# Score rounds of a fused attention and feed-forward block: two heads' plain scores beside two heads' lowered scores

## The chip, the cores and the metric

The kernel runs on one core of one Trainium2 chip. The core has five engines with a queue each: PE (matrix products into PSUM), DVE (vector work), ACT (activations), POOL (vector work[...]) and SP, which issues most of the transfers. The metric is the time of one execution in microseconds (us); lower is better. Times are medians of several executions.

## The reference

One block of a transformer in float32: four sequences (B) of 512 rows (T) of width 512 (D), 32 query heads of 16 columns that share 8 key and value heads, and a gated feed-forward layer of width 1376. Queries and keys are rotated by position, scores are causal, and the softmax is the usual one with its maximum taken off.

```python
q = q * cos + _rotate_half(q) * sin
k = k * cos + _rotate_half(k) * sin
att = jnp.einsum('bhgqd,bhkd->bhgqk', qg, k) / math.sqrt(D_HEAD)
att = jnp.where(causal, att, -jnp.inf)
probs = jax.nn.softmax(att, axis=-1)
ctx = jnp.einsum('bhgqk,bhkd->bhgqd', probs, v)
...
x = x + attention(_layernorm(x))          # with Wq, Wk, Wv, Wo
y = _layernorm(x)
x = x + (jax.nn.silu(y @ W_gate.T) * (y @ W_up.T)) @ W_down.T
```

Wq and Wk are drawn eight times larger than the other weights, so the scores are large and their maxima must be taken off before the exponential.

## The kernel before

**Groups.** The attention is cut into 32 groups of four heads (`GROUPS`, eight for each of the four sequences): pairs of groups (`hf` 0 and 1) share a tile of 128 query columns. The four heads of a group lie on partitions 0 to 31, 32 to 63, 64 to 95 and 96 to 127, so that their products, of 32 rows each, take separate quarters of PE. `masked(g)` (L436, POOL) makes the tile `qa[g]`: the group's rotated queries with one half of each 32 rows zeroed. The keys carry a row of ones in the zeroed half (L277), so whatever is written to that row of `qa` is added to each score of the query.

**Two passes over the scores.** The plain scores (L451, queries on the partitions of PSUM) serve to find each query's maximum. Their negatives are put into the spare row of `qa`, and the lowered scores (L549, keys on the partitions) then come out with the maximum already taken off. Exponentials (L556, ACT), a select that zeroes what lies above the diagonal (L560, POOL), and the products with the values (`averages`, L578) follow. The values carry ones beside them, so the sums of the softmax come out of the same products; `low_half`, `high_half`, `inverse` and `reciprocal` (L588 to L602) divide by them once per pair of groups.

**Rounds.** Four PSUM banks, one per head, are held as two tiles of two banks, `pairs`. A causal group of plain or lowered scores fits in two and a half fillings of them: 512 columns; 384 and 128; 256. So a group has five rounds: lowered 512, plain 512, lowered 384+128, plain 384+128, and last lowered 256 beside plain 256. The plain scores belong to a later group `h`, the lowered ones to the current group `g`. Lowered rounds are emptied by ACT (two exponentials of 1024 columns). In plain rounds DVE takes the maxima of heads 0 and 1 from PSUM (`from_bank`, L473, with the causal mask added), while ACT copies heads 2 and 3 to SBUF (L501), POOL masks the copy (L505) and DVE reduces it (L492, `from_copy`). In the last round DVE takes all four heads from PSUM, and the exponentials are issued after it.

**Two ways for the maxima.** For groups under `NEAR` = 9 the maxima go into the wide tiles `low`; `lowered(g)` turns them with four PE transposes (L524), and DVE adds them to `qa` (L525); `h` is then `g + 1`. From group 9 on they go into `packed`, are turned in 32x32 blocks by DVE (L531, `turned_round`), written to DRAM (L532) and read back into the spare rows of `qa` by four small transfers (L541, `laid_out`); `h` is then `g + 2`.

**What lies between the rounds.** Everything else is cut into steps of some 1.7 us of PE work: projections (L235, L290), output projection (L342), the feed-forward layer (L390, L416). `slot(b, steps)` runs the eight groups of one sequence and spreads the steps over the gaps between the rounds by shares written by hand. Slot 0 is filled with projections of later sequences only; slots 1 to 3 with output projections and feed-forward layers. Work that needs no PE stands in queues which the order of the code empties: `full` (what finishes a projection in slot 0: rotation on DVE and POOL, L243 to L246), `aside` (layer norm statistics, L187 to L195, and spreading of the keys), `later` (the divisions, on DVE) and `later_act` (`low_half`, on ACT). `thin` is true in slot 0. Before slot 0 come the first sequence's projections and the first group's plain scores, with query projections (`start[6:]`) and the second sequence's transposes (`turned1`, L207) between the rounds. POOL sets the spare parts of the value tiles there (L646) after `masked(0)` (L644).

The order of instructions is the order of the code (manual schedule); the tile framework adds the waits. Each engine runs its queue in order.

Of the kernel before, what the change touches and what calls it, by code (L numbers as in the profile page):

```python
# [48 lines left out]

NEAR = 9  # L50
# [26 lines left out]
def preln_block_kernel(  # L77
# [54 lines left out]
    low = [const.tile([P, NT, P], F32, name=f"low{hf}") for hf in range(2)]  # L132


    packed = [const.tile([P, 32], F32, name=f"packed{n}") for n in range(3)]
# [24 lines left out]
    sc = [pairs[r // 2][:, r % 2, :] for r in range(4)]  # L160
# [39 lines left out]
    def do(queue, n=1):  # L200
        for _ in range(min(n, len(queue))):
            queue.popleft()()
# [239 lines left out]
    def scores(g, at):  # L442

        if g >= len(GROUPS):
            return
        k = keys_of(g)
        for i, c in at:
            for r in range(4):
                rows = slice(32 * r, 32 * r + 32)
                n = P * (i + 1)  # L450
                nc.tensor.matmul(  # L451
                    sc[r][:, c : c + n], lhsT=qa[g][rows, ts(i, P)], rhs=k[rows, :n], start=True, stop=True
                )

    def greatest(g, at, lo, hi):


        if g >= len(GROUPS):
            return
        hf = GROUPS[g][2]  # L460

        def found(head, i):
            if g < NEAR:
                row = 32 * head + 16 * (1 - hf)
                return low[hf][:, i, row : row + 1]
            return packed[g % 3][:, NT * head + i : NT * head + i + 1]

        def from_bank(pair):
            for i, c in at:
                n = P * (i + 1)  # L470
                for r in range(2):
                    junk = work.tile([P, T], F32, tag="junk", name="junk")
                    nc.vector.tensor_tensor_reduce(  # L473
                        out=junk[:, :n],
                        in0=pairs[pair][:, r, c : c + n],
                        in1=mask[:, T - n :],
                        scale=-1.0,
                        scalar=BIG,
                        op0=ALU.add,
                        op1=ALU.min,  # L480
                        accum_out=found(2 * pair + r, i),
                    )

        def from_copy():
            for i, c in at:
                n = P * (i + 1)
                if g < NEAR:
                    row = 16 * (1 - hf)
                    dst = low[hf][:, i, :].rearrange("p (r k) -> p r k", k=32)[:, 2:4, row]
                else:  # L490
                    dst = packed[g % 3][:, 2 * NT : 4 * NT].rearrange("p (r i) -> p r i", i=NT)[:, :, i]
                nc.vector.tensor_reduce(  # L492
                    dst, copy[:, :, c : c + n], axis=mybir.AxisListType.X, op=ALU.max, negate=True
                )

        if lo > 0:
            from_bank(0)
            from_bank(1)
            return
        copy = work.tile([P, 2, T], F32, tag="copy", name="copy", bufs=2)  # L500
        nc.scalar.copy(copy, pairs[1])  # L501

        late = min(c + P * i for i, c in at)
        blocks = copy[:, :, late:hi].rearrange("p r (a k) -> p r a k", k=P)
        nc.gpsimd.affine_select(  # L505
            out=blocks,
            in_=blocks,
            compare_op=ALU.is_ge,
            fill=MASKED,
            base=0,  # L510
            pattern=[[0, 2], [0, (hi - late) // P], [-1, P]],
            channel_multiplier=1,
        )
        from_bank(0)
        do(full, len(full))
        from_copy()

    def lowered(g):

        if g >= len(GROUPS):  # L520
            return
        pt = bank()
        for i in range(NT):
            nc.tensor.transpose(pt[:, ts(i, P)], low[GROUPS[g][2]][:, i, :], ident)  # L524
        nc.vector.tensor_tensor(qa[g], qa[g], pt, ALU.add)  # L525

    def turned_round(g):
        if g >= len(GROUPS):
            return
        t = small.tile([P, 32], F32, tag="turned", name="turned", bufs=2)  # L530
        nc.vector.transpose(t, packed[g % 3])  # L531
        nc.sync.dma_start(out=lowest[g % 2], in_=t)  # L532
# [10 lines left out]
    def lowered_scores(g, at):  # L543

        k = keys_of(g)
        for j, c in at:
            for r in range(4):
                rows = slice(32 * r, 32 * r + 32)
                nc.tensor.matmul(  # L549
                    sc[r][:, c : c + T - P * j], lhsT=k[rows, ts(j, P)], rhs=qa[g][rows, P * j :], start=True, stop=True  # L550
                )

    def probabilities(at, e, width):

        for n in (1, 0):
            nc.scalar.activation(  # L556
                e[:, 2 * n : 2 * n + 2, :], pairs[n][:, :, :width], AF.Exp, scale=1.0 / math.sqrt(DH)
            )
        for j, c in at:
            nc.gpsimd.affine_select(  # L560
                out=e[:, :, c : c + P],
                in_=e[:, :, c : c + P],
                compare_op=ALU.is_ge,
                fill=0.0,
                base=0,
                pattern=[[0, 4], [1, P]],
                channel_multiplier=-1,
            )
# [64 lines left out]
    for t in (*low, *packed):  # L633
        nc.gpsimd.memset(t, 0.0)
# [15 lines left out]
    rounds = (((3, 0),), 0, T), (((2, 0), (0, 3 * P)), 0, T), (((1, 2 * P),), 2 * P, T)  # L650
    thin[0] = True
    for at, steps in zip(rounds, ([*start[6:8]], [*start[8:10]], [*turned1, *rest1[:2]])):
        scores(0, at[0])
        greatest(0, *at)
        do(full, len(full))
        for cost, step in steps:
            step()
    masked(1)
    lowered(0)
    for cost, step in start[10:]:  # L660
        step()

    def fill(steps, upto, done):
        while steps and done + steps[0][0] / 2 <= upto:
            cost, step = steps.popleft()
            step()
            done += cost
        return done

    def slot(b, steps):  # L670
# [5 lines left out]
        shares = 8 + 0.5 * (NEAR - 1 in groups)  # L676
        thin[0] = b == 0

        def gap(share):
            nonlocal done, part  # L680
            part += share / shares
            done = fill(steps, total * part, done)

        for g in groups:
            h = g + 1 if g + 1 < NEAR else g + 2
            if g % 8 == 7:
                do(aside, len(aside))
            lowered_scores(g, ((0, 0),))
            probabilities(((0, 0),), e0, T)
            if g + 1 > NEAR:  # L690
                laid_out(g + 1)
            do(later)
            if not thin[0]:
                do(aside)
            gap(0.17 if thin[0] else 0.19)
            if h == NEAR + 1:
                for at, lo, hi in rounds:
                    scores(NEAR, at)
                    greatest(NEAR, at, lo, hi)
                    gap(0.17)  # L700
                turned_round(NEAR)
                laid_out(NEAR)
            at, lo, hi = rounds[0]
            scores(h, at)
            greatest(h, at, lo, hi)
            do(aside)
            gap(0.15 if thin[0] else 0.17)
            lowered_scores(g, ((1, 0), (3, 3 * P)))
            probabilities(((1, 0), (3, 3 * P)), e1, T)
            do(later_act)  # L710
            do(later)
            if not thin[0]:
                do(aside)
            gap(0.17 if thin[0] else 0.19)
            at, lo, hi = rounds[1]
            scores(h, at)
            greatest(h, at, lo, hi)
            if thin[0]:
                do(aside)
            gap(0.17 if thin[0] else 0.2)  # L720
            at, lo, hi = rounds[2]
            lowered_scores(g, ((2, 0),))
            scores(h, at)
            greatest(h, at, lo, hi)
            if h > NEAR:
                turned_round(h)
            probabilities(((2, 0),), e2, 2 * P)
            if h == NEAR - 1:
                masked(NEAR)
                masked(NEAR + 1)  # L730
            elif h < NEAR:
                masked(g + 2)
            else:
                masked(g + 3)
            do(full, len(full))
            gap(0.17 if thin[0] else 0.25)
            averages(g)
            if h < NEAR:
                lowered(h)
            if thin[0]:  # L740
                do(aside)
                gap(0.17)
# [89 lines left out]
```

## Time and profile before

| | |
|---|---|
| median of 3 runs | 988.41 us (986.64 to 991.55) |
| profiled execution, its own time | 997.9 us |
| its span, first to last instruction | 996.2 us |
| mean granted PE clock | 0.969 |
| PE busy | 924.1 us (93%) |
| DVE busy | 492.4 us (49%) |
| ACT busy | 282.1 us (28%) |
| POOL busy | 246.6 us (25%) |
| maxima from PSUM, L473 | 320 instructions: 512 columns 691 ns, 384 557, 256 424, 128 291 |
| read of a maximum behind each | 83 ns |
| exponentials, L556 | 128 of 1024 columns, 1021 ns; 64 of 512, 594 ns |
| copy of two heads, L501 | 64, 1013 ns |
| mask of the copy, L505 | 64, 640 or 423 ns |
| reductions of the copy, L492 | 1024 elements 1222 ns, 768 954, 256 411 |
| transposes of the maxima, L524, and addition, L525 | 36 of 306 ns, 9 of 688 ns |
| reciprocals, L601 | 32, 1738 ns |

How to read it: the page cuts the span into 40 equal slices and gives each engine's busy share in tenths; PEclk is the clock that PE was granted. A group line has busy time and mean duration, then the idle time of the engine just before these instructions and what ended it. Matrix products are pipelined and run four at a time in the attention, so the sum of their durations is more than their busy time. An f32 product appears as two records. In the time line each line has start, duration, engine, source line, and in brackets the idle time before it with its releaser.

### The profile page before, as it was taken

To read this page: it belongs to the slowest core of one execution; us is meant where nothing else is said; L and a number is where in the kernel's file an instruction comes from. 1 tells how busy PE (TensorE), PEld (TensorE's weight loads), DVE (VectorE), ACT (ScalarE), POOL (GpSimd) and SP (SyncE) were. 2 spreads that over 40 slices of the span, in tenths; PEclk is the share of its full clock that TensorE was granted. 3 is DMA by queue.
4 is the path that set the end of the run, shared out by engine and by line. 5 is a ranking of instruction groups with operands and counts; after the bars stand their busy time and mean duration, and the time that the engine had idled before them with its cause. 6 is when DMAs were issued, how large, how long until landed. Compare 5 with 4: busy or idle time off the path is not lost.

```text
span 996.2 us, 12538 instructions
## 1 busy us (share of the span) xinstructions
PE 924.1 (93%) x4708; PEld 407.2 (41%) x4708; DVE 492.4 (49%) x1194; ACT 282.1 (28%) x359; POOL 246.6 (25%) x358
## 2 busy tenths in 40 slices
PE   6967876888989999999899999998999999999998
PEld 3443333335334344344444444444444434444443
DVE  7455556466746464554664545365555531512110
ACT  0223323343233433332233333323242422010000
POOL 5463443346231221122211111122111111100000
PEclk9998879798989999999999999999999999999999
DMA  6100100000024421013012111010112111022100
GB/s 211 43 1 1 43 1 1 1 1 1 3 64 160 158 58 46 24 53 130 12 55 65 44 40 43 22 44 12 54 44 65 39 44 54 21 74 75 47 11 32
DMA packets 62492, 47.18 MB, mean 47 GB/s; under 512 B 11520, under 2 KB 54528, under 8 KB 62176
## 3 DMA queue, kind: packets, MB, share of 16 engines
q1 hardware_dynamic: 62144, 40.62, 14.1%
q10 hardware_dynamic: 288, 5.77, 1.5%
q8 instruction: 37, 0.61, 0.3%
q14 instruction: 23, 0.19, 0.1%
HBM read 38.92 MB, written 7.45 MB: 47 GB/s over the span
## 4 chain that ended last, share of the span: by engine, by line
PE 82%; DVE 5%; issue 5%; ACT 4%; POOL 3%; DMA 0%; ACTq 0%; POOLq 0%; DVEq 0%
PE mm L390 30%; PE mm L416 14%; PE sc L549 9%; PE sc L451 8%; PE av L578 7%; PE mm L235 6%; PE mm L342 5%; ACT e L556 4%; DVE junk L473 2%; PE mm L207 1%; PE mm L290 1%; DVE st L187 1%; DVE rot L243 1%; PE mm L524 1%; POOL e L560 1%
## 5 line engine op out<-in xcount | busy, mean ns | idle before, releaser
L390 PE MATMUL mm<-xnT,shared 128*128 128x512 f32 (+1 forms) x704 | 322.7, 604 | 0.0
L556 ACT ACTIVATE e<-sc 128x1024 f32<-128x1024 f32 (+1 forms) x192 | 158.8, 879 | 372.1 <-PE sc L549 220.2
L473 DVE CUSTOM_DVE_ANT_0 junk<-sc,mask 128x256 f32<-128x256 f32 (+3 forms) x320 | 152.7, 477 | 154.2 <-PE sc L451 126.8
L390 PEld LDWEIGHTS mm<-xnT,shared 128*128 128x128 f32 (+1 forms) x704 | 126.3, 188 | 164.5 <-issue 155.5
L560 POOL TENSOR_SCALAR_AFFINE_SELECT e<-e 128x512 f32<-128x512 f32 x128 | 80.3, 638 | 417.1 <-ACT e L556 184.6
L416 PE MATMUL mm<-wd_sb,home 128*128 128x512 f32 (+1 forms) x352 | 159.6, 600 | 0.0
L549 PE MATMUL sc<-qa,home 32*128 32x512 f32 (+3 forms) x1024 | 99.9, 483 | 15.6 <-DVE low L473 13.6
L451 PE MATMUL sc<-home,qa 32*128 32x512 f32 (+3 forms) x1024 | 95.8, 466 | 18.2 <-ACT e L556 16.3
L501 ACT COPY copy<-sc 128x1024 f32<-128x1024 f32 x64 | 64.8, 1013 | 119.1 <-PE sc L451 109.5
L416 PEld LDWEIGHTS mm<-wd_sb,home 128*128 128x128 f32 (+1 forms) x352 | 64.6, 190 | 82.8 <-issue 81.4
L578 PE MATMUL av<-e,home 128*32 128x512 f32 (+3 forms) x1024 | 79.7, 448 | 15.4 <-POOL e L560 15.4
L399 DVE SCALAR_TENSOR_TENSOR g<-g,mm 128x512 f32<-128x512 f32 (+1 forms) x44 | 30.2, 686 | 100.4 <-ACT g L398 100.4
L549 PEld LDWEIGHTS sc<-qa,home 32*128 32x128 f32 x1024 | 44.7, 190 | 83.7 <-issue 22.1
L451 PEld LDWEIGHTS sc<-home,qa 32*128 32x128 f32 x1024 | 47.3, 187 | 74.7 <-issue 27.8
L235 PE MATMUL mm<-xnT,shared 128*128 128x512 f32 x120 | 64.2, 675 | 0.8 <-issue 0.8
L505 POOL TENSOR_SCALAR_AFFINE_SELECT copy<-copy 128x256 f32<-128x256 f32 x64 | 34.0, 531 | 114.2 <-ACT copy L501 114.2
L401 DVE TENSOR_TENSOR home<-mm,g 128x512 f32<-128x512 f32 (+1 forms) x44 | 30.2, 686 | 61.6 <-PE mm L390 61.6
L492 DVE TENSOR_REDUCE packed<-copy 128x2 f32<-128x1024 f32 (+2 forms) x69 | 57.5, 862 | 5.0 <-POOL copy L505 3.0
L342 PE MATMUL mm<-wo_sb,cx 128*128 128x512 f32 x128 | 59.4, 605 | 0.0
L578 PEld LDWEIGHTS av<-e,home 128*32 128x32 f32 x1024 | 28.6, 111 | 72.7 <-issue 46.2
L601 DVE RECIPROCAL inv<-inv 128x256 f32<-128x256 f32 x32 | 55.3, 1738 | 0.1
L398 ACT ACTIVATE g<-mm 128x512 f32<-128x512 f32 (+1 forms) x44 | 26.4, 599 | 97.4 <-PE mm L390 97.4
(75 smaller groups left out, 552.6 us busy)
## 6 DMA issues: line engine op xcount, KB each, us to landing
shared<-in_wg SPq DMA_DIRECT2D x40, 256.0 KB
shared<-in_wu SPq DMA_DIRECT2D x40, 256.0 KB
xr<-in_x SPq DMA_DIRECT2D x16, 256.0 KB
out<-xr SPq DMA_DIRECT2D x16, 256.0 KB
xa<-in_x SPq DMA_DIRECT2D x12, 256.0 KB
spill<-wd_sb ACTq DMA_DIRECT2D x1, 2816.0 KB
home<-spill ACTq DMA_DIRECT2D x1, 2816.0 KB
wd_sb<-in_wd SPq DMA_DIRECT2D x1, 2560.0 KB
```

The costliest lines, as they stand in the source:

```text
L235: nc.tensor.matmul(ps, lhsT=w[:, k, ts(m, P)], rhs=xnT[:, k, :], start=k == 0, stop=k == NK - 1)
L342: nc.tensor.matmul(ps, lhsT=cx[m][:, ts(i, P)], rhs=wo_sb[:, m, :], start=m == 0, stop=m == 3)
L390: nc.tensor.matmul(ps[:m, :], lhsT=wgu[c][:, a, k, :m], rhs=xnTs[""][:, k, :], start=k == 0, stop=k == NK - 1)
L416: nc.tensor.matmul(py[i], lhsT=homes[n][:m, f, ts(i, P)], rhs=wd_sb[:m, f, :], start=f == 0, stop=f == NF - 1)
L451: nc.tensor.matmul(sc[r][:, c : c + n], lhsT=qa[g][rows, ts(i, P)], rhs=k[rows, :n], start=True, stop=True)
L473: nc.vector.tensor_tensor_reduce(out=junk[:, :n], in0=pairs[pair][:, r, c : c + n], in1=mask[:, T - n :], scale=-1.0, scalar=BIG, op0=ALU.add,
L492: nc.vector.tensor_reduce(dst, copy[:, :, c : c + n], axis=mybir.AxisListType.X, op=ALU.max, negate=True)
L501: nc.scalar.copy(copy, pairs[1])
L549: nc.tensor.matmul(sc[r][:, c : c + T - P * j], lhsT=k[rows, ts(j, P)], rhs=qa[g][rows, P * j :], start=True, stop=True)
L556: nc.scalar.activation(e[:, 2 * n : 2 * n + 2, :], pairs[n][:, :, :width], AF.Exp, scale=1.0 / math.sqrt(DH))
L560: nc.gpsimd.affine_select(out=e[:, :, c : c + P], in_=e[:, :, c : c + P], compare_op=ALU.is_ge, fill=0.0, base=0, pattern=[[0, 4], [1, P]] ...
L578: nc.tensor.matmul(av[32 * r : 32 * r + 32, P * j :], lhsT=v[:, j, 4 * (m // 2) + r, DH * (1 - hf) : DH * (3 - hf)], rhs=e[:, r, c : c + n ...
```

## The change

All groups now use the way through DRAM: `NEAR`, `lowered`, the wide `low` tiles, and the copying of heads 2 and 3 are gone; `packed` is renamed `low`. `h` is `g + 2` for every group, so the plain scores of both groups 0 and 1 are found before slot 0.

The rounds are mixed. `plain` and `less` are the two pairs of banks. In each of four visits two heads of group `h` have plain scores in `plain`, and the other two heads of group `g` have lowered scores in `less`: 512 columns for one half of the heads and then the other, and the same with 384 and 128. One exponential empties `less`, DVE's maxima (`greatest`) empty `plain`. In the fifth, `last_visit`, each bank holds 256 lowered columns and 256 plain ones, issued head by head; the exponentials are now issued ahead of the maxima. The last two groups have no `h`, and use both pairs for lowered scores.

The shares of the steps are equal: a fortieth of the slot in each of five gaps a group. In slots 1 to 3 `fill` also takes one entry of `aside` after each step. Two steps of the second sequence's queries move from slot 0 to before it, and two of the fourth sequence's move from slot 1 to slot 0. `masked(0)` at L644 is left as it is.

```diff
-    low = [const.tile([P, NT, P], F32, name=f"low{hf}") for hf in range(2)]
-    packed = [const.tile([P, 32], F32, name=f"packed{n}") for n in range(3)]
+    low = [const.tile([P, 32], F32, name=f"low{n}") for n in range(3)]
...
-    sc = [pairs[r // 2][:, r % 2, :] for r in range(4)]
+    plain, less = pairs
...
+    def both_scores(h, g, visit):
+        for c, i, j, heads in visit:
+            for r in heads:
+                if h < len(GROUPS):
+                    plain_score(h, r, i, plain[:, r % 2, c : c + P * (i + 1)])
+                else:
+                    less_score(g, r, j, plain[:, r % 2, c : c + T - P * j])
+            for r in (2, 3) if heads[0] == 0 else (0, 1):
+                less_score(g, r, j, less[:, r % 2, c : c + T - P * j])
+
+    def greatest(g, r, i, src):
+        n = P * (i + 1)
+        junk = work.tile([P, T], F32, tag="junk", name="junk")
+        nc.vector.tensor_tensor_reduce(
+            out=junk[:, :n],
+            in0=src,
+            in1=mask[:, T - n :],
+            scale=-1.0,
+            scalar=BIG,
+            op0=ALU.add,
+            op1=ALU.min,
+            accum_out=low[g % 3][:, NT * r + i : NT * r + i + 1],
+        )
+
+    def all_greatest(h, visit):
+        if h < len(GROUPS):
+            for c, i, j, heads in visit:
+                for r in heads:
+                    greatest(h, r, i, plain[:, r % 2, c : c + P * (i + 1)])
+        do(full, len(full))
+
+    def last_visit(h, g):
+        for r in range(4):
+            if h < len(GROUPS):
+                plain_score(h, r, 1, pairs[r // 2][:, r % 2, 2 * P :])
+            less_score(g, r, 2, pairs[r // 2][:, r % 2, : 2 * P])
+        for n in (1, 0):
+            exponentials(e2[:, 2 * n : 2 * n + 2, :], pairs[n][:, :, : 2 * P])
+        causal(e2, 0)
+        masked(g + 3)
+        if h < len(GROUPS):
             for r in range(4):
...
+                greatest(h, r, 1, pairs[r // 2][:, r % 2, 2 * P :])
         do(full, len(full))
...
-    rounds = (((3, 0),), 0, T), (((2, 0), (0, 3 * P)), 0, T), (((1, 2 * P),), 2 * P, T)
+    low_heads, high_heads = (0, 1), (2, 3)
+    visits = (
+        ((0, 3, 0, low_heads),),
+        ((0, 3, 0, high_heads),),
+        ((0, 2, 1, low_heads), (3 * P, 0, 3, low_heads)),
+        ((0, 2, 1, high_heads), (3 * P, 0, 3, high_heads)),
+    )
     thin[0] = True
...
+    shares = [2, 2, 2, 5, 2, 1]
+    opening = deque([*start[6:], *turned1, *rest1[:4]])
+    for h in range(2):
+        masked(h)
+        for entries in (((0, 3),), ((0, 2), (3 * P, 0)), ((0, 1),)):
+            for c, i in entries:
+                for r in range(4):
+                    plain_score(h, r, i, pairs[r // 2][:, r % 2, c : c + P * (i + 1)])
+            for r in range(4):
+                for c, i in entries:
+                    greatest(h, r, i, pairs[r // 2][:, r % 2, c : c + P * (i + 1)])
+            do(full, len(full))
+            for _ in range(shares.pop(0)):
+                opening.popleft()[1]()
+        turned_round(h)
+        if h == 0:
+            laid_out(0)
+    masked(2)
...
             done += cost
+            if not thin[0]:
+                do(aside)
...
         for g in groups:
-            h = g + 1 if g + 1 < NEAR else g + 2
+            h = g + 2
             if g % 8 == 7:
                 do(aside, len(aside))
...
+            laid_out(g + 1)
+            for n, visit in enumerate(visits):
+                e = (e0, e0, e1, e1)[n]
+                if h < len(GROUPS):
+                    both_scores(h, g, visit)
+                    exponentials(e[:, slice(0, 2) if n % 2 else slice(2, 4), :], less)
+                elif n % 2 == 0:
+                    both_scores(h, g, visit)
+                    exponentials(e[:, 2:4, :], less)
+                    exponentials(e[:, 0:2, :], plain)
+                if n == 1:
+                    causal(e0, 0)
+                if n == 3:
+                    causal(e1, 0)
+                    causal(e1, 3 * P)
+                all_greatest(h, visit)
+                if n == 2:
+                    do(later_act)
+                if n in (0, 1, 3):
+                    do(later)
+                if n in (0, 2):
+                    do(aside)
+                gap()
+            last_visit(h, g)
+            turned_round(h)
             do(aside)
+            gap()
             averages(g)
...
-    slot(0, [begin2, *rest1[2:], *turned2, begin3, *rest2, *turned3, *rest3[:-6]])
+    slot(0, [begin2, *rest1[4:], *turned2, begin3, *rest2, *turned3, *rest3[:-4]])
```

`plain_score` and `less_score` issue one product each, as L451 and L549 did; `exponentials` and `causal` are the two halves of the former `probabilities` (L556, L560); `turned_round`, `laid_out`, `masked` and `averages` keep their work.

More of the change, by code (lines that the diff above doesn't have):

```diff
@@ L48 @@
 SWAP = [(d + 16) % 32 for d in range(32)]
-NEAR = 9
 GROUPS = [(b, m, hf) for b in range(B) for m in range(4) for hf in range(2)]
@@ L440, in keys_of @@
         return homes[HOME[b]][:, 4 + 2 * (m // 2) + hf, :]
[L442 to L447, printed above, removed]
-            for r in range(4):
[L449 to L514, printed above, removed]
-        do(full, len(full))
-        from_copy()
@@ L518, in lowered, with rows_of, plain_score @@
[L518 to L525, printed above, removed]
+    def rows_of(r):
+        return slice(32 * r, 32 * r + 32)
+    def plain_score(g, r, i, dst):
+        k = keys_of(g)[rows_of(r), : P * (i + 1)]
+        nc.tensor.matmul(dst, lhsT=qa[g][rows_of(r), ts(i, P)], rhs=k, start=True, stop=True)
@@ new lines, in less_score @@
+    def less_score(g, r, j, dst):
+        k = keys_of(g)[rows_of(r), ts(j, P)]
+        nc.tensor.matmul(dst, lhsT=k, rhs=qa[g][rows_of(r), P * j :], start=True, stop=True)
+    def both_scores(h, g, visit):
[7 more added lines that the diff above has]
+                less_score(g, r, j, less[:, r % 2, c : c + T - P * j])
@@ L530, in turned_round @@
         t = small.tile([P, 32], F32, tag="turned", name="turned", bufs=2)
-        nc.vector.transpose(t, packed[g % 3])
+        nc.vector.transpose(t, low[g % 3])
         nc.sync.dma_start(out=lowest[g % 2], in_=t)
@@ L541, in laid_out, with exponentials, causal @@
             nc.sync.dma_start(out=rows[:, i], in_=src[i])
[L543 to L568, printed above, removed]
+    def exponentials(dst, src):
+        nc.scalar.activation(dst, src, AF.Exp, scale=1.0 / math.sqrt(DH))
+    def causal(e, c):
+        nc.gpsimd.affine_select(
+            out=e[:, :, c : c + P],
+            in_=e[:, :, c : c + P],
+            compare_op=ALU.is_ge,
+            fill=0.0,
+            base=0,
+            pattern=[[0, 4], [1, P]],
+            channel_multiplier=-1,
+        )
     us = {}
@@ L632, in preln_block_kernel @@
     load_w(wo_sb, wo)
-    for t in (*low, *packed):
+    for t in low:
         nc.gpsimd.memset(t, 0.0)
@@ L648, in preln_block_kernel @@
         step()
-    rounds = (((3, 0),), 0, T), (((2, 0), (0, 3 * P)), 0, T), (((1, 2 * P),), 2 * P, T)
-    thin[0] = True
[L652 to L661, printed above, removed]
+    low_heads, high_heads = (0, 1), (2, 3)
[4 more added lines that the diff above has]
+        ((0, 2, 1, high_heads), (3 * P, 0, 3, high_heads)),
+    )
+    thin[0] = True
+    shares = [2, 2, 2, 5, 2, 1]
[16 more added lines that the diff above has]
+    masked(2)
     def fill(steps, upto, done):
@@ L675, in slot, with gap @@
         groups = range(8 * b, 8 * b + 8)
-        shares = 8 + 0.5 * (NEAR - 1 in groups)
         thin[0] = b == 0
-        def gap(share):
+        def gap():
             nonlocal done, part
-            part += share / shares
-            done = fill(steps, total * part, done)
+            part += total / 40
+            done = fill(steps, part, done)
         for g in groups:
-            h = g + 1 if g + 1 < NEAR else g + 2
+            h = g + 2
             if g % 8 == 7:
                 do(aside, len(aside))
[L688 to L705, printed above, removed]
-            do(aside)
[L707 to L736, printed above, removed]
-            averages(g)
[L738 to L742, printed above, removed]
@@ L778, in preln_block_kernel @@
             before[0],
-            *rest3[-6:-4],
+            *rest3[-4:-2],
             *before[1:],
-            *rest3[-4:],
+            *rest3[-2:],
             firsts,
```

## The prediction

> **What bounds the kernel now.** I read the forty slices of the page first, then a table by stretch, then the time line inside a stretch.
>
> ```profile
> PE   6967876888989999999899999998999999999998
> PEclk9998879798989999999999999999999999999999
> 47.40:236.90 189.50, 145.32 (x1006) 70.57 (x1006) 106.70 (x285) 65.48 (x82) 86.34 (x109) 0.88 0.02 6
> 300.00:836.00 536.00, 527.76 (x2856) 221.48 (x2855) 278.13 (x670) 182.24 (x230) 110.47 (x178) 0.99 0.19 57
> ```
>
> Columns of the table: length, busy PE, PEld, DVE, ACT, POOL, granted clock, DMA share, GB/s. From 300 us on PE is busy 98% at full clock: there only PE work counts, and DVE (52%) and ACT (34%) follow it. Slot 0 (groups 0 to 7, 47.4 to 239.5 us by the starts of the 512-column L549 products in the time line: 24.0 us a group) is different: no engine is busy over 77%, and the clock is 0.88. It is a chain of waits. The waits of PE in slot 0, and one last round of it:
>
> ```profile
> PE av L578 <- POOL e L560: 15.4, 7, 4.9
> PE sc L549 <- DVE low L473: 13.6, 8, 2.0
> PE sc L451 <- ACT e L556: 13.2, 12, 2.2
> ```
> ```profile
> 163.95 0.42 DVE L473 CUSTOM_DVE_ANT_0 junk<-sc,mask 128x256 f32<-128x256 f32 x1
> ...
> 166.00 1.08 ACT L556 ACTIVATE e<-sc 128x512 f32<-128x512 f32 x2 [4.96 <-DVE low L473]
> ...
> 167.16 0.64 POOL L560 TENSOR_SCALAR_AFFINE_SELECT e<-e 128x512 f32<-128x512 f32 x1 [2.72 <-ACT e L556]
> ...
> 167.85 0.64 PE L578 MATMUL av<-e,home 128*32 128x256 f32 x8 [1.51 <-POOL e L560]
> ```
>
> Each line starts with start and duration. The last round's exponentials stand behind all its maxima, the diagonal select behind them, the last averages behind that: PE pays 15.4 us in the slot. The other 27 us are rounds waiting for the four banks, by turns for two exponentials and for maxima.
>
> **Slot 0, a group.** Old chain, from one round's products to the next: after the plain-lowered round 1.1 + two exponentials 1.94 and 0.1 of signalling = 3.2; the first maxima 2.85 (products 1.1, two 0.69 maxima with reads of 0.08, signals); second exponentials 3.25; second maxima 3.2; last round 1.15 + maxima 2.0 + exponentials 1.1 + select 0.65, then the closing averages 0.6, with signals 5.9; transposes L524, the addition L525 (0.69) and a filler 2.5. Sum 20.9; measured 24.0, so 3.1 go to lumps in DVE's and POOL's queues and to the clock.
>
> New chain: each visit has one exponential (1.02, ACT) beside two heads' maxima (DVE), so the maxima set it: 2.85 for the first two visits; 3.2 for the next two (two 384 and two 128 columns, 1.76 as at 159.53, plus products 1.15). The last visit's exponentials now come ahead of its maxima: products 1.15, a filler of 1.85, averages 2.5, with the select done about 2.0 after the products, ahead of its averages. The maxima start 1.2 later (the old row shows that ACT and DVE don't read these banks together) and end 3.4 after the products, under filler and averages. L524 and L525 go (0.6 us of PE, 0.69 of DVE). Sum 17.6. DVE's total hardly grows: the copied heads' reductions (1.22 + 0.95 + 0.41) become maxima from PSUM (2 x 0.69, 0.56, 0.29 and six reads of 0.08 = 3.6), +1.0 a group; minus L525, plus L531 (0.21): about 13.9 of 20 us. ACT loses 2.0 (L501), POOL 1.06 (L505); nobody waits for these outside slot 0, so there they bring nothing.
>
> What covers less: in the old order high_half and inverse (L592, L593, L597: 2.2) and each reciprocal (1.74) ran while ACT held the round. Now each visit waits for DVE and leaves it about 1.4, so a group with a finished pair pays some 1.2 (0.6 a mean group), normalisations and rotations 0.7, POOL's backlog ahead of the select 0.5. That and the clock's slow products (8.1 us of PE in the chain, +0.9) give 20.3; the old excess of 3.1 on 17.6 gives 20.7. I take 20.5: 8 x 20.5 = 164 against 192.1.
>
> A rule speaks to the clock. Row: group 96.3 to 120.4 had no PE wait over 2.1 us, and 0.79 granted; 195.8 to 215.5 had none over 1.6 and 1.00. The Trainium skill (TensorE: Matmul & The Clock Gate, "Why this matters for your kernels") asks only for no idle gap over about 3 us. By the rule most of slot 0 would already run full, and shorter gaps bring no clock; by the row only groups near 1.5 us of wait do. My waits stay near 1 to 2, so I keep about 0.9. By full clock the group would be 19.6, 7 us less in the slot.
>
> **Before slot 0.** This part pays. The masked(0) at L644 stays, and the new loop calls masked(0) again, behind the three memsets.
>
> ```profile
> 25.90 0.69 POOL L436 TENSOR_SCALAR qa<-home,rope_sb 128x512 f32<-128x512 f32 x1
> 26.53 2.70 POOL L646 MEMSET home<- 128x1536 f32 x2
> 26.64 1.14 PE L451 MATMUL sc<-home,qa 32*128 32x512 f32 x8 [0.81 <-POOL qa L436]
> 29.16 1.38 POOL L646 MEMSET wd_sb<- 128x1536 f32 x1
> ```
>
> The first scores wait for that second qa: 30.5 + 0.69, so 31.3 for 26.6, and PE idles 5 us with nothing to cover it; the clock that slot 0 loses after 2 us waits will be lost here too, so I put the first products at double time. Then, step by step: round one of group 0 with two steps (3.7) to 38.0; round two 1.15 + 3.7 to 42.9; round three and 3.7 to 47.3. Group 1's qa stands on POOL behind the rotation of the second queries, done on DVE only after round three's maxima: 50.2. Round one with turned1 and half the keys (3.1 + 1.85) to 56.3, round two to 61.2, round three 0.6 + 1.85 to 63.7. Slot 0's first visit needs qa of group 2, behind the keys' rotation: 68, for 47.4: +20.6. Bounds: PE's work alone from 31.3 (two groups' rounds 5.9, steps 21.6) would end at 59; I take the stepwise value as both POOL queues are written out. SP's queue: one turned and four laid_out transfers per group, now also for 0 to 8. In the trace L541 waits 25.7 us for turned's landing in 17 waits, 1.5 each, and each set is issued a group (20 us) ahead of its use; begin3's loads ahead of them wait only for transposes just issued. Nothing; without that cover, 1.5 a group.
>
> Start of slot 1: 68 + 164 = 232, for 239.5: -7.5.
>
> **Slots 1 to 3.** Two query halves (3.7) and one group's scores (2.9) have moved ahead: -6.6. Transposes wait for a burst of normalisations:
>
> ```profile
> PE mm L207 <- DVE xn L195: 9.6, 4, 4.5
> ```
>
> Now fill pops one after every step, so these are done when the transposes come: -8. Against that, at three slot ends the whole pair (2.2 + 2 x 1.74 = 5.7 us of DVE) is issued right ahead of a visit that waits for DVE: averages' end + 5.7 + 1.45 against products 1.1 and filler 3.05: +3 each, +8 with a filler sometimes left between. In the old order ACT's round lay there. In steady groups a gap is a fifth of about 3.05 x 5 us; one in five has a single step (1.85), about 0.2 short of the maxima and 1 us short where a reciprocal stands ahead: +3 in 24 groups, of which the old shows 0.3 us a group. Net -3.6.
>
> One unknown: the last visit issues plain and lowered products of one head together, head by head, not four heads in turn. Each f32 product is two records.
>
> ```profile
> 134.60:134.65 0.05, 0.05 (x4) 1.00 0.00 0
> 134.65:134.70 0.05, 0.05 (x8) 1.00 0.00 0
> 134.33 0.71 PE L549 MATMUL sc<-qa,home 32*128 32x256 f32 x8
> ```
>
> Eight records of four heads, two per head in program order, yet four start together and four 0.3 us later. These can only be one of each head, so a head's second pass doesn't hold up the next head. The skill (same page, "Part 3: Packing small matmuls") has matmuls start and end in strict program order. By the rule the new order would put each head's four passes (0.216 each at 161.95) in a row: 3.5 us for 1.15, +2.4 a group, +60 us. The row sits nearer: 0, at most some tenths a group.
>
> **Sum.** -7.5 - 3.6 = -11 on a span of 996.2, run time 997.9: 986.8. The median shown is 0.95% under that run, so 977 us.
>
> **Rivals.** (1) Slot 0 becomes dense: 18.6 us a group (chain plus 1, full clock) and a start at 59: 59 + 149 = 208, -31.5 - 3.6, gives 954. For it: DVE has room, and group 195.8 to 215.5 took 19.7 even now. Against: POOL's queue before slot 0. (2) No gain: 22 us a group, as each visit now hangs on DVE; the start eats it: 244, +4.5 - 3.6, gives 989. (3) Slower: DVE's lumps reach PE in slots 1 to 3. Place: the single-step gaps after a reciprocal or pair; price 1.1 us a group for the 0.13 above, over 24 groups +23, so 1000; it decides from 0.6 a group. For it: these slots have no slack on PE at all; against: DVE at 52%, and two-step gaps of 3.7 for maxima of 1.8. (4) The row-group order of the last visit costs +60: 1036. The change does what it says: no group keeps L501, L505 or L524.
>
> **Chances.** Forecast 0.42, (1) 0.20, (2) 0.20, (3) 0.13, (4) 0.05. The range 955 to 999 leaves out (4), part of (1) and half of (3): 0.2. The forecast's own range is 968 to 984. About 0.5% (5 us) can be told from nothing: faster 0.61 (forecast nearly whole, (1)), same 0.20, slower 0.19.
>
> **What would show it.** Steps: L578's wait for POOL in slot 0 falls from 15.4 to under 5; the first L451 product (its new line) starts near 31 with a wait for qa; slot 0's first visit near 68 and the groups 20 to 21 us apart; L207's wait under 3; DVE junk named as releaser of score products at slot ends. Wrong, if slot 0's groups stay at 23 or more, if the first visit comes before 60, or if PE is idle over 2% between 300 and 800.

## The result, and the profile after

The changed kernel takes 981.9 us (median of 12 runs, 980.0 to 987.91), the kernel before 991.65 (12 runs beside it): a ratio of 0.9914, with a 95% interval of 0.9892 to 0.9936. It is faster by a little under one per cent; the forecast was 977, a ratio of 0.988. The profiled runs of these two kernels, at 987.65 and 997.9 us, are each some 6 us above their medians, while those of the experiments lie within 3 us of theirs, so a profile of an experiment beside that of the changed kernel shows up to 6 us more gain, or less loss, than the medians do.

The span of the profiled execution fell from 996.2 to 985.9 us. Three stretches, cut where the time line shows the first 512-column lowered product of group 0 and of group 8, show where it went:

| stretch | before | after | difference | forecast |
|---|---|---|---|---|
| ahead of slot 0 | 47.4 | 71.2 | +23.8 | +20.6 |
| slot 0, eight groups | 192.1 | 166.3 | -25.8 | -28 |
| slots 1 to 3 and the tail | 756.7 | 748.4 | -8.3 | -3.6 |
| span | 996.2 | 985.9 | -10.3 | -11 |

So slot 0 won most of what it was meant to win, and the opening gave nearly all of it back. Of the last 8.3 us, 6.3 are work that was only moved into the opening: PE's busy time in slot 1 falls from 196.4 to 190.1 us, and slot 1 from 203.9 to 195.1. Slot 2 stays at 203.5 us, and what follows it at some 349.5. From the page of the kernel after, the rows of the 40 slices; then from a table by stretch (length, busy PE, PEld, DVE, ACT, POOL, granted clock, DMA share, GB/s) slot 0 and the same 536 us as before:

```profile
PE   6777878878999999999999999999999999999998
PEclk9889897999999999999999999999999999999999
...
71.00:237.50 166.50, 136.22 (x984) 66.27 (x984) 109.53 (x356) 51.46 (x67) 71.67 (x88) 0.91 0.05 15
300.00:836.00 536.00, 529.64 (x2856) 223.80 (x2855) 286.44 (x837) 144.92 (x187) 89.03 (x137) 0.99 0.18 54
```

In slot 0 PE is busy 82% of the time for 77% before, at 0.91 of the clock for 0.88. DVE is the only engine that works more, ACT and POOL work less. In the later stretch PE's busy time hardly moved (528 to 530 us); DVE works more there (278 to 286), ACT (182 to 145) and POOL (110 to 89) less, and PE is busy 99% for 98%. The new limit of slot 0 is in the waits of PE (times of a wait: total, number, longest), first over slot 0, then over groups 8 to 31:

```profile
PE sc L444 <- DVE low L467: 28.3, 15, 4.2
PE sc L444 <- POOL qa L432: 3.8, 1, 3.8
```
```profile
PE sc L444 <- DVE low L467: 7.7, 4, 2.8
PE mm L203 <- DVE xnT L206: 2.1, 3, 1.2
```

The averages no longer wait for POOL (15.4 us before), and no round waits for ACT (13.2 in slot 0). In their place every wait of the scores (L444) but that for a query tile is for DVE's maxima (L467). A last visit in the time line shows how the gate opened:

```profile
105.29 0.74 PE L444 MATMUL sc<-home,qa 32*128 32x256 f32 x8
...
105.83 0.63 PE L449 MATMUL sc<-qa,home 32*128 32x256 f32 x8
...
106.66 1.09 ACT L517 ACTIVATE e<-sc 128x512 f32<-128x512 f32 x2 [2.12 <-PE sc L449]
...
107.78 0.42 DVE L467 CUSTOM_DVE_ANT_0 junk<-sc,mask 128x256 f32<-128x256 f32 x1 [1.32 <-ACT e L517]
...
108.30 2.36 PE L539 MATMUL av<-e,home 128*32 128x512 f32 x32
...
108.55 0.63 POOL L521 TENSOR_SCALAR_AFFINE_SELECT e<-e 128x512 f32<-128x512 f32 x1
```

All 32 records of the averages run on without a break: the select that they need ends at 109.2, before the last eight are due. The maxima wait 1.3 us for the exponentials, under filler and averages. The two PE lines also settle the row-group question, beside the second line of the same round before (the first, at 134.33, stands in the prediction):

```profile
134.87 0.61 PE L451 MATMUL sc<-home,qa 32*128 32x256 f32 x8
```

The sixteen records of the changed kernel end at 106.46, 1.17 us after the first, for 1.15 before.

The opening, from the time line of PE, with its three waits for a query tile:

```profile
31.86 2.09 PE L444 MATMUL sc<-home,qa 32*128 32x512 f32 x8 [6.18 <-POOL qa L432]
...
51.18 2.09 PE L444 MATMUL sc<-home,qa 32*128 32x512 f32 x8 [2.75 <-POOL qa L432]
...
71.00 1.11 PE L444 MATMUL sc<-home,qa 32*128 32x512 f32 x2 [3.79 <-POOL qa L432]
```

The first products after the first two waits take 2.09 us for the 1.14 that they took before: the wait is paid, and then the clock. It stood at half for 6.8 us around each of them (length, busy PE with the records in the stretch, granted clock, DMA share, GB/s):

```profile
30.20:37.00 6.80, 5.14 (x12) 0.50 0.00 0
50.70:57.50 6.80, 5.78 (x24) 0.50 0.01 1
```

### The profile page after: what moved, and what is told of

It is laid out like the page before. It is cut to its first block, busy times and chain, and to the rows that moved or that the text cites. A ratio compares the mean times of both kernels' runs of the same rounds, so it can differ in the third digit from the quotient of the medians.

```text
span 985.9 us, 12673 instructions
## 1 busy us (share of the span) xinstructions
PE 918.1 (93%) x4672; PEld 403.6 (41%) x4672; DVE 511.1 (52%) x1482; ACT 225.2 (23%) x295; POOL 212.7 (22%) x293
## 4 chain that ended last, share of the span: by engine, by line
PE 85%; DVE 10%; POOL 2%; issue 1%; ACT 1%; DMA 0%; SPq 0%; DVEq 0%; ACTq 0%; POOLq 0%
PE mm L386 32%; PE mm L412 15%; PE sc L444 15%; PE av L539 7%; PE mm L338 6%; PE mm L231 5%; DVE junk L467 4%; PE sc L449 3%; PE mm L286 1%; DVE inv L562 1%; PE mm L203 1%; DVE rot L239 1%; DVE xa L191 1%; DVE st L183 1%; POOL rot L240 1%
## 5 line engine op out<-in xcount | busy, mean ns | idle before, releaser
L467 DVE CUSTOM_DVE_ANT_0 junk<-sc,mask 128x128 f32<-128x128 f32 (+3 forms) x512 | 250.7, 490 | 228.7 <-PE sc L449 131.6
L517 ACT ACTIVATE e<-sc 128x1024 f32<-128x1024 f32 (+1 forms) x192 | 165.4, 881 | 508.0 <-PE sc L449 508.0
L444 PE MATMUL sc<-home,qa 32*128 32x512 f32 (+3 forms) x1024 | 171.5, 486 | 48.8 <-DVE low L467 36.0
L449 PE MATMUL sc<-qa,home 32*128 32x512 f32 (+3 forms) x1024 | 166.4, 469 | 0.0
L444 PEld LDWEIGHTS sc<-home,qa 32*128 32x128 f32 x1024 | 74.2, 189 | 169.9 <-DVE low L467 67.7
L449 PEld LDWEIGHTS sc<-qa,home 32*128 32x128 f32 x1024 | 77.0, 189 | 4.4 <-issue 3.9
L338 PE MATMUL mm<-wo_sb,cx 128*128 128x512 f32 x128 | 62.3, 632 | 0.0
L416 DVE SCALAR_TENSOR_TENSOR xr<-mm,xr 128x512 f32<-128x512 f32 x16 | 10.9, 684 | 73.4 <-PE mm L412 73.4
L467 DVE DVE_READ_ACCUMULATOR2_ANT low<- 128x1 f32 x512 | 42.3, 83 | 0.0
L186 POOL TENSOR_TENSOR rstd<-rstd,neghalf 128x1 f32<-128x1 f32 x32 | 22.8, 713 | 88.3 <-DVE rstd L185 82.8
```

Of the source, the lines that this page charges most:

```text
L338: nc.tensor.matmul(ps, lhsT=cx[m][:, ts(i, P)], rhs=wo_sb[:, m, :], start=m == 0, stop=m == 3)
L444: nc.tensor.matmul(dst, lhsT=qa[g][rows_of(r), ts(i, P)], rhs=k, start=True, stop=True)
L449: nc.tensor.matmul(dst, lhsT=k, rhs=qa[g][rows_of(r), P * j :], start=True, stop=True)
L467: nc.vector.tensor_tensor_reduce(out=junk[:, :n], in0=src, in1=mask[:, T - n :], scale=-1.0, scalar=BIG, op0=ALU.add, op1=ALU.min, accum_o ...
L517: nc.scalar.activation(dst, src, AF.Exp, scale=1.0 / math.sqrt(DH))
```

## The experiments

Each is the changed kernel with the edit shown, and has a short name, e1 to e8. Ratios are to the kernel before, with 95% intervals; the changed kernel stands at 0.9914.

**The second masked(0) (e1).**

```diff
     for h in range(2):
-        masked(h)
+        if h:
+            masked(h)
```

> The second masked(0), behind the three memsets, is left out. My theory (PE waits 6.2 us for that tile, with nothing to cover it, and the products after it run at the slower clock): the first score products start near 26.6 us for 31.9, slot 0 starts 5 to 7 us earlier than 71, and the whole is 5 to 7 us shorter than the changed kernel, about 0.986 of the kernel before. Rival (what is won at the front is lost again, because the queues of DVE and POOL set the end of the opening): slot 0 still starts at 69 to 71 and the time stays at 0.991.

Measured: 975.76 us, 0.9831 (0.9807 to 0.9855). Slot 0 starts at 63.0 for 71.2, and PE's wait at the first scores is 1.1 us for 6.2, by its time line:

```profile
27.10 1.14 PE L444 MATMUL sc<-home,qa 32*128 32x512 f32 x8 [1.11 <-POOL qa L432]
...
62.95 1.22 PE L449 MATMUL sc<-qa,home 32*128 32x512 f32 x2
```

What was won reaches the end: one instruction of 0.69 us behind three memsets cost about 8 us of the opening in the profile, and 6 us by the medians or 8 by the ratios. The rival falls. What exceeds the wait itself (5.1 us) fits the clock: in this profile the first half-clock stretch comes at 44.6 us, in the changed kernel's one lies from 30 to 37.

**All three query tiles early (e2).**

```diff
     masked(0)
+    masked(1)
     for n in range(1, 4):
...
     for h in range(2):
-        masked(h)
...
             do(full, len(full))
+            if h == 0 and len(entries) == 2:
+                masked(2)
...
-    masked(2)
```

> As e1, and the query tiles of groups 1 and 2 are made as soon as their rotated queries are there, ahead of the memsets and of later rotations in POOL's queue. My theory (POOL's place for these tiles costs 6.2 + 2.75 + 3.8 us of PE waits in the opening): all three waits go, slot 0 starts 11 to 15 us earlier, near 58, and the time is about 0.978 of the kernel before. Rival (DVE's maxima bound the opening: 17.8 us of them for two groups): slot 0 starts at 63 or later and the time is 0.985 or more.

Measured: 965.54 us, 0.9734 (0.9707 to 0.9762). Time line of PE:

```profile
26.98 1.14 PE L444 MATMUL sc<-home,qa 32*128 32x512 f32 x8 [1.25 <-POOL qa L432]
...
41.00 1.14 PE L444 MATMUL sc<-home,qa 32*128 32x512 f32 x8
...
54.73 0.70 PE L444 MATMUL sc<-home,qa 32*128 32x512 f32 x2
```

Group 1's scores and slot 0's first visit start with no wait, 16.3 us earlier in all than in the changed kernel, and the products take their 1.14 us again. DVE's maxima, the rival, hold up nothing: the work of both groups fits beside PE. The opening is still 7.3 us longer than before (54.7 for 47.4), about the 6.6 us of PE work that moved into it. The rest of the opening's loss was POOL's queue and the clock behind it.

**Maxima ahead of the exponentials, as before (e3).**

```diff
-        for n in (1, 0):
-            exponentials(e2[:, 2 * n : 2 * n + 2, :], pairs[n][:, :, : 2 * P])
-        causal(e2, 0)
-        masked(g + 3)
         if h < len(GROUPS):
             for r in range(4):
                 greatest(h, r, 1, pairs[r // 2][:, r % 2, 2 * P :])
+        for n in (1, 0):
+            exponentials(e2[:, 2 * n : 2 * n + 2, :], pairs[n][:, :, : 2 * P])
+        causal(e2, 0)
+        masked(g + 3)
         do(full, len(full))
```

> In the last visit the maxima come ahead of the exponentials again, as before the change; all else as changed. My theory (the exponentials and the select behind them gated the last averages in slot 0, at 15.4 us before): the waits of the averages for POOL come back with 8 to 15 us in slot 0, little of it offset by maxima that end 1.2 us sooner, none in slots 1 to 3; the time rises by 8 to 14 us over the changed kernel, to about 1.001 of the kernel before. Rival (the wait had gone because POOL has less to do without the mask of the copies): under 4 us come back, 0.991 to 0.995.

Measured: 997.82 us, 1.0067 (1.0041 to 1.0093): this one swap is worth more than the whole change brings. But not as I had placed it. The waits of PE over slot 0, then over groups 8 to 31:

```profile
PE av L539 <- POOL e L521: 5.3, 6, 2.4
```
```profile
PE av L539 <- POOL e L521: 3.9, 7, 1.3
```

In slot 0 the averages wait 5.3 us again, not 8 to 15, and the slot is 171.8 us for 166.3. More appears in slots 1 to 3 and the tail (755.3 us for 748.4), where I had expected none. Slot 0 of the changed kernel, then of e3 (length, busy PE with the records, granted clock, DMA share, GB/s):

```profile
71.20:237.50 166.30, 136.03 (x984) 0.91 0.05 15
```
```profile
69.00:240.80 171.80, 134.53 (x986) 0.94 0.05 14
```

PE is idle for 7 us more (37.3 for 30.3), but at a higher clock: by 0.91 and 0.94 the changed kernel's profile lost some 4 to 5 us more to it in this slot (an estimate: 0.09 of 166.3 us for 0.06 of 171.8). So the profiles show less of the swap (10.2 us of span) than the medians (15.9). The mechanism holds, with the rival's share (a lighter POOL) plausible for the part of the 15.4 us that doesn't come back; no run takes the two apart. Nor does one take apart what is left of slot 0's gain, 20.3 us even with the swap, between the mixed rounds and the way through DRAM.

**No aside work in the filler (e4).**

```diff
             done += cost
-            if not thin[0]:
-                do(aside)
```

> The filler of slots 1 to 3 takes no entry of the aside queue after each step. My theory (this, and not the new rounds, ended the burst of normalisations that the transposes waited for): the transposes wait 7 to 10 us in slots 1 to 3 again, for about 3 now, and the time rises by 6 to 8 us over the changed kernel, to about 0.998 of the kernel before. Rival (the new order of the rounds took the wait away): no change, 0.991.

Measured: 989.49 us, 0.9976 (0.9958 to 0.9993), as expected in the time. Waits of PE in groups 8 to 31:

```profile
PE mm L203 <- DVE xn L191: 5.2, 2, 2.9
```

The two waits lie in slot 1, whose group 9 grows from 26.6 to 32.9 us, at a granted clock of 0.84 for 0.94, so that waits and clock share the growth. With the transposes' waits for copies out of PSUM (1.8 us in the same view) they make 7.0, the low end of what was expected. In slots 2 and 3 no transpose waits for a normalisation, and for copies only 0.9 us each, though the waits were 2.3 each before the change. So the pops in `fill` end slot 1's burst; what ended the other two wasn't tried.

**The first maxima twice (e5).**

```diff
                     greatest(h, r, i, plain[:, r % 2, c : c + P * (i + 1)])
+                    if i == 3:
+                        greatest(h, r, i, plain[:, r % 2, c : c + P * (i + 1)])
```

> The changed kernel with each 512-column maximum of the first two visits taken twice: 1.5 us more of DVE in each of two visits a group. My theory (in slot 0 the maxima are what each visit waits for; in slots 1 to 3 they lie under the filler): slot 0 grows by 2.4 to 3.1 us a group, 20 to 25 us in all, and slots 1 to 3 by 0 to 10 us; the time is 1.012 to 1.026 of the kernel before. Rival A (ACT, POOL and PE set the visits as much as DVE): slot 0 grows by under 8 us. Rival B (DVE has no room beside PE in slots 1 to 3 either): these grow by over 20 us.

Measured: 1030.67 us, 1.040 (1.0356 to 1.0444). Slot 0 takes 192.2 us for 166.3, +25.9, just above the 20 to 25, for 22.7 us more of DVE (132.2 for 109.5): DVE's maxima are its chain, and rival A falls. But slots 1 to 3 and the tail grow by 18.2, where I had expected 10 at most. Slot 0 as a stretch, as for e3; waits of PE over slot 0, then over groups 8 to 31:

```profile
69.00:261.20 192.20, 148.71 (x988) 0.83 0.04 13
```

```profile
PE sc L444 <- DVE low L467: 41.5, 18, 5.2
```
```profile
PE sc L444 <- DVE low L467: 23.2, 16, 4.2
```

Of slot 0's growth 13.2 us are idle time of PE; the rest is PE busy for longer, at 0.83 of the clock for 0.91. In the later groups there are sixteen waits for four: the filler covers the maxima as they are, but not 1.5 us more. Between my 10 and rival B's 20, it is nearer to rival B: the room beside PE is narrow.

**A gap of filler at the start of slots 1 to 3 (e6).**

```diff
-            part += total / 40
+            part += total / (41 if b else 40)
...
+        if b:
+            gap()
         for g in groups:
```

> The changed kernel with a forty-first gap of filler at the start of slots 1 to 3, between the divisions flushed at the slot's end and the first visit. My theory (5.7 us of DVE work stand ahead of that visit's maxima, and PE waits 2.8 + 2.4 + 2.4 us for them): these three waits shrink to under 1 us each and the time falls by 5 to 8 us, to about 0.985 of the kernel before. Rival (the waits only move one visit on, since DVE stays as late): no change, 0.991.

Measured: 969.2 us, 0.9784 (0.9747 to 0.9822), 13 us below the changed kernel, for the 5 to 8 expected. The waits of PE in slots 1 to 3 are these:

```profile
PE sc L444 <- DVE low L467: 3.2, 6, 2.1
PE mm L203 <- ACT xnT L208: 0.7, 3, 0.2
```

Two of the three waits shrink to 0.3 us; the first is 2.1 for 2.8, where under 1 had been expected. The 3.4 us that transposes and the product behind them waited for transposed rows to be copied out of PSUM fell to 0.7. That is about 7 us of waits. The rest fits the clock, as the changed kernel shows at the start of slot 2, first in its time line of PE, then in a table by stretch (length, busy PE with the records in the stretch, granted clock, DMA share, GB/s):

```profile
439.75 1.21 PE L444 MATMUL sc<-home,qa 32*128 32x512 f32 x2 [2.39 <-DVE low L467]
```
```profile
436.00:439.80 3.80, 1.41 (x8) 1.00 0.89 378
439.80:443.20 3.40, 3.40 (x10) 0.50 0.91 386
443.20:447.00 3.80, 3.80 (x23) 1.00 0.60 229
```

The wait of 2.39 us is followed by 3.4 us at half clock, which is 1.7 us of products lost again. The changed kernel has four such stretches from group 8 to the last scores, 13.6 us together, so some 6.8 lost; with the gap there is none, and the granted clock from 234.9 to 811.5 is 1.00. But a half-clock stretch doesn't follow such a wait each time. At the start of slot 3 code and wait are the same in the changed kernel and in e1; each time the line of PE, then the stretch behind it:

```profile
643.25 0.70 PE L444 MATMUL sc<-home,qa 32*128 32x512 f32 x2 [2.38 <-DVE low L467]
```
```profile
644.60:648.00 3.40, 3.40 (x5) 0.50 0.00 0
```
```profile
633.41 0.70 PE L444 MATMUL sc<-home,qa 32*128 32x512 f32 x2 [2.38 <-DVE low L467]
```
```profile
633.40:640.20 6.80, 6.79 (x35) 1.00 0.01 3
```

**Both edits (e7), and one more (e8).** First e2 and e6 together; then, added to them, the keys' spreading in another queue:

```diff
-                    aside.appendleft(spread)
+                    full.append(spread)
```

> The early query tiles of e2 and the gap of e6 together. My theory (they lie in different stretches): the gains add, about 0.967 of the kernel before. Rival: the second gain is gone beside the first, 0.973.

> As e7, and the spreading of a sequence's keys goes into the queue of finishing work instead of to the head of the aside queue, so that its shuffle on DVE is issued one visit after the rotation that it waits for on POOL, not right behind it with the next maxima queued after. My theory (DVE stands 2.2 us at that shuffle, three times in slot 0, with the maxima behind it): slot 0 shrinks by 3 to 6 us against e7, about 0.962 of the kernel before. Rival (something else in DVE's queue is late next): under 2 us.

Measured: 955.14 us, 0.9635 (0.9599 to 0.967), and 954.31 us, 0.9624 (0.9589 to 0.9659). The two gains nearly add (26.8 us by the medians, for 16.4 and 12.7 alone), and both versions beat both kernels; e7 is 3.7% under the kernel before and 2.8% under the changed one (0.9635 / 0.9914). The spreading is inconclusive: in the profile slot 0 is 2.5 us shorter (167.7 for 170.2), PE's waits for maxima fall from 31.6 to 27.7 us, but one wait of averages for POOL of 2.7 us is new, the clock there is 0.92 for 0.90, which alone could be worth those 2.5 us, and the times can't be told apart.

## Why the prediction was right

Point by point, by its steps. **The sum**, -11 us forecast and -10.3 measured on the span, came closer than its terms: the opening cost 3.2 us more and slot 0 won 2.2 less than forecast, and slots 1 to 3 gave 4.7 more. That these cancel is luck.

**The chain of slot 0** held. 20.8 us a group was measured for 20.5, as a mean of groups from 19 to 23.5. The exponentials no longer stand behind the maxima, the averages no longer behind POOL, and DVE is the one engine that the visits wait for, which doubling its first maxima confirms (+25.9 us). The swap back (e3) shows the exponentials' place at work, with less of it in slot 0 than forecast in its profile.

**The opening** held in every part: the second query tile came at 31.9 (31.3 forecast), group 1's at 51.2 (50.2), slot 0 at 71 (68). The three missing microseconds fit the clock: I gave the first products double time once, and the profile has two stretches of 6.8 us at half clock. e1 and e2 show that the cause is the place in POOL's queue; PE's work alone, which I had as the other bound at 27.7 us from the first scores, is what e2 reaches: 26.98 to 54.73.

**The slot ends** were forecast at 3 us each; they were 2.8, 2.4 and 2.4 of waiting, and in this profile each was followed by a half-clock stretch. e6 shows the cause.

**The transposes' burst** went from 9.6 us of waits to about 3. Its cause is shown for slot 1 only (e4). In slots 2 and 3 the transposes gained 2.3 us each and the slot ends took 2.4 each, so these slots end as long as before.

**The wrong term** is that of steady groups in slots 1 to 3: +3 us forecast, from single-step gaps that would be short of the maxima. From group 10 on PE waits hardly at all outside the slot ends, and waits that I hadn't counted are gone, 3.1 us of the plain rounds for ACT among them. In the kernel before, over groups 8 to 31:

```profile
PE sc L451 <- ACT e L556: 3.1, 12, 0.3
```

The forecast had PE's idle time from group 8 on rise by 3 us (-8 for the transposes, +8 for the slot ends, +3 for the steady groups); it fell by 2.7, from 17.8 to 15.1. These 5.7 us, less 1 us of busy time (it fell by 5.6 us, for the 6.6 of work moved away), are the 4.7 us by which this stretch beat the forecast. e5 shows how near the term was to being real: 1.5 us more on DVE in two visits of five cost 18 us there.

**The clock.** It was granted at 0.91 in slot 0, for the 0.9 that I kept. The case stands nearer to the row than to the rule of the Trainium skill that the prediction names (TensorE: Matmul & The Clock Gate, "Why this matters for your kernels"), which asks for no idle gap over about 3 us: waits of 2.4 us were followed by 3.4 us at half clock, though not everywhere. But I read the row too narrowly. The half clock that begins the group at 96.3 (6.5 us, until 102.8) comes behind a wait of 2.7 us that ends at 94.3, in the group ahead of it, so the 0.79 can't be put down to waits of 2.1 us alone.

**The order of products** stands by the row: head by head costs 1.17 us for 1.15, so rival (4) is out. Rival (1), a dense slot 0, didn't come about: e7 reaches 955 us, at the 954 forecast for it, but by a short opening and clean slot ends, not by slot 0, which kept its 20 to 21 us a group (21.3 by a cut that counts the new gap of filler in). Rivals (2) and (3) fell; e5 shows what (3) would have looked like.

## What to carry to other kernels

When groups of work are brought forward, follow each small instruction that they need through its engine's queue, not only its duration: one of 0.69 us, behind three memsets, cost 6 to 8 us, because nothing covered the wait. When a row of visits is moved from two engines to one, look for the places where that engine's other work comes in a lump, and put independent filler there. And count a wait of PE here at its length and, where a half-clock stretch follows, half of that stretch more: 2.4 us and 1.7 at the start of slot 2.

## What the runs showed of the hardware

At the starts of slots 2 and 3 of the changed kernel a wait of PE of 2.4 us was followed by 3.4 us at half the granted clock. The same wait at the start of slot 3 left the clock whole in e1, e2 and e4, so the length of the wait alone doesn't decide it; what does stays open. Shorter waits went both ways too: one of 1.91 us in group 1 was followed by half clock from 98.5 to 101.9 us in the changed kernel, and by none in e1. So in slot 0 the same program code had 20.6, 22.0 and 24.0 us for groups 1 to 3 in e7, and 19.2, 20.3 and 24.2 in e2, with the half-clock stretches in other places. A change in one stretch so moves a later one by a few microseconds that its own instructions don't explain. Products on different quarters of PE's rows didn't wait for each other's order here: with four records of one head issued ahead of the next head's, sixteen records took 0.02 us more than in turns.
